# Last image's dynamic filters: one branch of five added up by VectorE in PSUM, its taps spread among the others

## The chip, the cores and the metric

The kernel runs on one core of a Trainium2 chip. The time is that of one execution on the device, in microseconds (us). PE is TensorE (PEld its weight loads), DVE VectorE, ACT ScalarE, POOL GpSimd. SBUF and PSUM are the two on-chip memories of this kernel; its matmuls write to PSUM. The granted clock is TensorE's clock as a share of full speed, as the profile records it; "half clock" is 0.5.

## The reference, cut to what matters

Four images of 256 x 48 x 48 pass through two layers. Layer 0 is a convolution with attention and is not touched. Layer 1 makes, from a 3x3 convolution, 45 weights per pixel (5 branches of 9, a softmax over each 9), and each branch sums nine shifted copies of its input, called taps, under these weights:

```python
for i, d in enumerate((1, 6, 12, 24, 36)):
    w = jax.nn.softmax(guidance[:, 9 * i:9 * (i + 1)], axis=1)
    outs.append(_dyn_branch(x, w, d))      # sum over 9 taps: shifted x * w[:, k]
cat = jnp.concatenate(outs, axis=1)
y = _conv(cat, W_scale, pad=0)             # 1x1, 6*256 -> 256; then batch norm
```

## The kernel before

An image is worked through in six chunks of 8 rows. Each tap takes three engines. TensorE broadcasts the tap's weights over 128 partitions into a PSUM buffer `wb` (a ring of three). VectorE multiplies it with the shifted input into `prod` (a ring of five). POOL adds `prod` to the branch's sum `cat`. When a branch is done, its **mix**, the part of the 1x1 convolution that reads it, is queued and issued on TensorE some six taps later. (The code is cut: `...` and some arguments, `name=` above all, are left out.)

```python
for n in range(len(DILATIONS)):
    cat = work1.tile([P, NH, CH], F32, tag="cat", bufs=CATS)             # CATS = 4
    for k, oy, ox, y0, y1, x0, x1 in taps_of(c, n):
        pw = ps_w.tile([P, 512], F32, tag="w")                           # bufs=3
        nc.tensor.matmul(pw[:, : nr * WW], pick[:, k : k + 1].to_broadcast([2 * NG, P]),
                         w[:, l0 * WW : l1 * WW], start=True, stop=True)
        if k % 9 == 4:
            nc.vector.tensor_tensor(accv, wb, src, ALU.mult)             # first tap, into cat
        else:
            prod = work1.tile([P, NH, CH], F32, tag="prod", bufs=PRODS)  # PRODS = 5
            nc.vector.tensor_tensor(pv, wb, src, ALU.mult)
            nc.gpsimd.tensor_tensor(dst, dst, pv, ALU.add)
        ...
        pump()            # issues queued TensorE work: mixes, guidance steps, layer 0
    for o in range(NH):   # one queue entry for each output half
        queue.append((tap + PRODS + 1, mix(c, n + 1, o, lambda i, cat=cat: cat[:, i, :])))

def pump():
    while owed > 0:
        if queue and queue[0][0] <= tap:
            owed -= queue.pop(0)[1]()
            continue
        ...               # else a guidance step of the next chunks, else layer 0
```

A mix is four matmuls, which the trace shows as eight records. In the timelines shown here each engine works through its instructions in the order in which the kernel issued them, so one that waits or takes long holds up those behind it (as the mix of 4.54 us below does). Layer 1 of images 0 to 2 runs beside layer 0 of the next image; that of image 3 runs alone at the end of the program.

## Time and profile before

| | before |
|---|---|
| median of 3 runs when the prediction was made | 3422.59 us (3419.55 to 3422.88) |
| span of the profiled run | 3419.3 us |
| last image's loop, first POOL add to last `y` copy | 283.8 us |
| busy in it: POOL, PE, DVE | 258, 230, 177 us |

I measure "the loop" between two marks in the timeline: the start of POOL's first add and the start of ScalarE's copy of the sixth `y`. (The 281 us of the prediction leave out the last mix; its 231 and 179 us of PE and DVE are those of a window a little longer than the loop.) The start of the loop differs by up to 11 us between profiles of unchanged earlier code, so one profile's loop is compared, not its start or end.

The prediction shows that POOL is the busy engine there.

```profile
3212.94 4.54 PE L990 MATMUL py<-cat,wsc 128*128 128x384 f32 x8 [1.95 <-POOL cat L1060]
```
```profile
3212.92 0.76 DVE L1058 TENSOR_TENSOR prod<-wb,pad 128x576 f32<-128x576 f32 x1 [0.81 <-POOL cat L1060]
3217.76 0.76 DVE L1058 TENSOR_TENSOR prod<-wb,pad 128x576 f32<-128x576 f32 x1 [4.08 <-PE wb L1035]
```

TensorE was in a mix of 4.54 us, made no broadcast, and VectorE stood still for 4.08 us. POOL did not notice: its line of fourteen merged adds runs from 3199.75 to 3222.06 us without a break, on the products waiting in its ring.

### The profile page before, as it was taken

To read this page: it belongs to the slowest core of one execution; us is meant where nothing else is said; L and a number is where in the kernel's file an instruction comes from. 1 tells how busy PE (TensorE), PEld (TensorE's weight loads), DVE (VectorE), ACT (ScalarE), POOL (GpSimd) and SP (SyncE) were. 2 spreads that over 40 slices of the span, in tenths; PEclk is the share of its full clock that TensorE was granted. 3 is DMA by queue.
4 is the path that set the end of the run, shared out by engine and by line. 5 is a ranking of instruction groups with operands and counts; after the bars stand their busy time and mean duration, and the time that the engine had idled before them with its cause. 6 is when DMAs were issued, how large, how long until landed. Compare 5 with 4: busy or idle time off the path is not lost. (4 is left out here: it accounts for less than half of the span.)

```text
span 3419.3 us, 45333 instructions
## 1 busy us (share of the span) xinstructions
PE 3158.2 (92%) x17814; PEld 1363.3 (40%) x17814; DVE 2377.3 (70%) x2837; ACT 1471.5 (43%) x1739; POOL 1041.5 (30%) x793
## 2 busy tenths in 40 slices
PE   7999999999989999999998999999998999987873
PEld 4542222445652222345563222245565222233442
DVE  2059899455659898836557899955555999876655
ACT  0067777300118777600024777730011887750002
POOL 0000000068770000037783000007786000007994
PEclk9999999999999999999999999999999999998876
DMA  3110000000002000000003000000000100022004
GB/s 119 29 27 6 6 10 6 15 24 5 10 14 52 6 6 10 11 28 10 5 10 61 6 6 10 6 6 5 5 10 16 23 6 6 10 81 100 10 5 176
DMA packets 70973, 81.52 MB, mean 24 GB/s; under 512 B 51280, under 2 KB 62048, under 8 KB 67680
## 3 DMA queue, kind: packets, MB, share of 16 engines
q1 hardware_dynamic: 69952, 73.15, 7.5%
q0 software_dynamic: 800, 5.41, 0.4%
q8 instruction: 141, 2.31, 0.3%
q14 instruction: 80, 0.66, 0.1%
HBM read 50.23 MB, written 28.31 MB: 23 GB/s over the span
## 5 line engine op out<-in xcount | busy, mean ns | idle before, releaser
L1060 POOL TENSOR_TENSOR cat<-cat,prod 128x768 f32<-128x768 f32 (+7 forms) x768 | 1034.1, 1352 | 2330.1 <-DVE prod L1058 2288.0
L721 ACT ACTIVATE p<-se 128x1024 f32<-128x1024 f32 (+1 forms) x1440 | 1273.6, 937 | 377.2 <-PE se L709 341.0
L754 DVE TENSOR_TENSOR acc<-acc,p 128x1024 f32<-128x1024 f32 (+1 forms) x1200 | 1250.5, 1112 | 42.0 <-ACT p L721 41.1
L709 PE MATMUL se<-q,k 32*128 32x512 f32 (+1 forms) x5760 | 830.5, 602 | 15.8 <-ACT p L721 12.6
L1058 DVE TENSOR_TENSOR prod<-wb,pad 128x768 f32<-128x768 f32 (+7 forms) x768 | 560.5, 750 | 404.4 <-PE wb L1035 369.8
L737 PE MATMUL num<-p,vT 128*32 128x512 f32 (+1 forms) x5760 | 716.6, 568 | 35.4 <-DVE no L757 35.4
L631 PE MATMUL pc<-pad,wc 128*128 128x384 f32 x1728 | 624.1, 494 | 2.3 <-issue 2.3
L1035 PE MATMUL wb<-w,pick 90*128 90x384 f32 (+3 forms) x888 | 478.7, 563 | 58.6 <-DVE prod L1058 52.2
L709 PEld LDWEIGHTS se<-q,k 32*128 32x128 f32 x5760 | 285.1, 184 | 565.2 <-issue 452.7
L631 PEld LDWEIGHTS pc<-pad,wc 128*128 128x128 f32 x1728 | 317.7, 191 | 219.1 <-issue 47.7
L990 PE MATMUL py<-cat,wsc 128*128 128x384 f32 x960 | 365.9, 511 | 16.7 <-POOL cat L1060 16.7
L737 PEld LDWEIGHTS num<-p,vT 128*32 128x32 f32 x5760 | 114.8, 108 | 529.5 <-issue 464.2
L640 ACT ACTIVATE hid<-pc,bn_t_f,bn_s_f 128x384 f32<-128x384 f32 x48 | 32.2, 672 | 614.5 <-PE pc L631 614.5
L1035 PEld LDWEIGHTS wb<-w,pick 90*128 90x128 f32 x888 | 172.3, 197 | 220.2 <-DVE prod L1058 101.6
L990 PEld LDWEIGHTS py<-cat,wsc 128*128 128x128 f32 x960 | 187.2, 200 | 127.4 <-POOL cat L1060 22.9
L875 PE MATMUL pg<-pad,wcat 128*45 128x384 f32 x864 | 173.1, 514 | 2.5 <-DVE pad L585 2.2
L1050 DVE TENSOR_TENSOR cat<-wb,pad 128x768 f32<-128x768 f32 x120 | 114.6, 955 | 86.9 <-PE wb L1035 86.3
L1005 ACT COPY y<-py 128x768 f32<-128x768 f32 x24 | 19.2, 799 | 317.4 <-PE py L990 317.4
L651 PE MATMUL pq<-hid,wqkv 128*128 128x384 f32 x384 | 135.0, 486 | 0.0
L679 DVE TENSOR_REDUCE qm<-q 128x1 f32<-128x2304 f32 x8 | 20.4, 2546 | 156.6 <-ACT q L658 156.5
L812 PE MATMUL pp<-ao,wp 128*128 128x384 f32 x192 | 82.2, 559 | 38.0 <-DVE pad L820 37.1
L754 DVE TENSOR_TENSOR acc<-p,p 128x1024 f32<-128x1024 f32 (+1 forms) x80 | 85.8, 1115 | 32.2 <-ACT p L721 32.2
(115 smaller groups left out, 1085.1 us busy)
## 6 DMA issues: line engine op xcount, KB each, us to landing
pad<-in_x SPq DMA_DIRECT2D x14, 1152.0 KB, 14.7
x_d<-pad SPq DMA_DIRECT2D x48, 192.0 KB, 2.5
y_d<-y SPq DMA_DIRECT2D x24, 384.0 KB, 2.7
xst<-in_x SPq DMA_DIRECT2D x18, 384.0 KB, 3.9
y<-y_d SPq DMA_DIRECT2D x3, 2304.0 KB, 19.6
out<-y SPq DMA_DIRECT2D x6, 1152.0 KB, 12.6
x<-x_d SPq DMA_DIRECT2D x2, 2304.0 KB, 24.2
x_first<-in_x SPq DMA_DIRECT2D x2, 1152.0 KB, 7.3
```

Source lines behind the costliest of these rows:

```text
L631: nc.tensor.matmul(pc[:, :CH], wc[:, i, k, o * P : (o + 1) * P], window(gn, i, c * R, k // 3 - 1, k % 3 - 1), start=(i == 0 and k == 0), s ...
L651: nc.tensor.matmul(pq[:, :CH], wqkv[:, i, s, g * P : (g + 1) * P], hid[:, i, cols], start=(i == 0), stop=(i == NH - 1),)
L709: nc.tensor.matmul(ss[j // 2][:, j % 2, :n], k_[r, g, m * P : (m + 1) * P], q[r, g, q0 : q0 + n], start=True, stop=True,)
L721: nc.scalar.activation(p[:, :, :n], ss[pair][:, :, :n], AF.Exp, scale=QS)
L737: nc.tensor.matmul(st["num"][r, :n], vT[:, m, g * P + j * D : g * P + (j + 1) * D], ps[j // 2][:, j % 2, :n], start=(m == 0), stop=(m == N ...
L754: nc.vector.tensor_tensor(a, other, ps[pair][:, :, :n], ALU.add)
L875: nc.tensor.matmul(pg[64 * s : 64 * s + NG, :CH], wcat[:, i, k, :], window(gn, i, (c + s) * R, k // 3 - 1, k % 3 - 1), start=(i == 0 and k ...
L990: nc.tensor.matmul(py[c][:, o, :CH], wsc[:, n * NH + i, o * P : (o + 1) * P], rhs(i), start=(n == 0 and i == 0), stop=(n == len(DILATIONS) ...
L1035: nc.tensor.matmul(pw[:, : nr * WW], pick[:, k : k + 1].to_broadcast([2 * NG, P]), w[:, l0 * WW : l1 * WW], start=True, stop=True,)
L1050: nc.vector.tensor_tensor(accv, wb, src, ALU.mult)
L1058: nc.vector.tensor_tensor(pv, wb, src, ALU.mult)
L1060: nc.gpsimd.tensor_tensor(dst, dst, pv, ALU.add)
```

## The change

Its intent is to relieve POOL in the last image only. Branch 1 (dilation 6) is summed by VectorE in a PSUM accumulator, which ScalarE copies to `cat` at the end, and its nine taps are spread evenly among those of the other branches, so that the two adders work side by side. The core of the diff:

```diff
+        def spread(taps, own):
+            rest = [(n, i) for n in taps if n not in own for i in range(len(taps[n]))]
+            mine = [(n, i) for n in taps if n in own for i in range(len(taps[n]))]
+            both = [((i + 0.5) / len(t), t[i]) for t in (rest, mine) for i in range(len(t))]
+            return [t for _, t in sorted(both)]
...
-                for n in range(len(DILATIONS)):
...
+                own = {1} if b == B - 1 else set()
+                taps = {n: list(taps_of(c, n)) for n in range(len(DILATIONS))}
+                order = spread(taps, own)
+                for n, at in order:
...
+                        acc = cat
+                        if n in own:
+                            acc = ps_c.tile(
+                                [P, 2, 512], F32, tag="acc", name=f"acc_{b}_{c}", bufs=1
+                            )
...
-                            nc.gpsimd.tensor_tensor(dst, dst, pv, ALU.add)
+                        eng = nc.vector if n in own else nc.gpsimd
+                        eng.tensor_tensor(dst, dst, pv, ALU.add)
...
+                        if n in own:
+                            nc.scalar.copy(cat, acc[:, :, :CH])
```

More of the change, by code (lines that the diff above doesn't have):

```diff
@@ L849, in dynamic_filters @@
         def dynamic_filters(b, ao, chunk, norm, other, pools):
-            ps_w, ps_y, ps_m, work1 = pools
+            ps_c, ps_w, ps_y, ps_m, work1 = pools
             gn = pads[b % 2]
@@ L983, in pump, with mix @@
                     owed -= got
-            def mix(c, n, o, rhs):
+            def mix(c, n, o, rhs, last=False):
                 def go():
@@ L994, in go @@
                             start=(n == 0 and i == 0),
-                            stop=(n == len(DILATIONS) and i == NH - 1),
+                            stop=(last and i == NH - 1),
                         )
-                    if n == len(DILATIONS) and o == NH - 1:
+                    if last and o == NH - 1:
                         done(c)
@@ L1025, in dynamic_filters @@
                 w = ready[c]
-                for n in range(len(DILATIONS)):
-                    cat = work1.tile(
-                        [P, NH, CH], F32, tag="cat", name=f"cat_{b}_{c}_{n}", bufs=CATS
-                    )
-                    accv = cat.rearrange("p h (r w) -> p h r w", w=WW)
-                    for k, oy, ox, y0, y1, x0, x1 in taps_of(c, n):
-                        nr, ncol = y1 - y0, x1 - x0
-                        l0, l1 = y0 - c * R, y1 - c * R
-                        pw = ps_w.tile([P, 512], F32, tag="w", name=f"wb_{b}_{c}_{k}")
-                        nc.tensor.matmul(
-                            pw[:, : nr * WW],
-                            pick[:, k : k + 1].to_broadcast([2 * NG, P]),
-                            w[:, l0 * WW : l1 * WW],
-                            start=True,
-                            stop=True,
-                        )
-                        wb = (
-                            pw[:, : nr * WW]
-                            .rearrange("p (r w) -> p r w", w=WW)[:, :, x0:x1]
-                            .unsqueeze(1)
-                            .to_broadcast([P, NH, nr, ncol])
-                        )
-                        src = gn[:, :, 1 + y0 + oy : 1 + y1 + oy, 1 + x0 + ox : 1 + x1 + ox]
-                        if k % 9 == 4:
-                            nc.vector.tensor_tensor(accv, wb, src, ALU.mult)
-                        else:
-                            prod = work1.tile(
-                                [P, NH, CH], F32, tag="prod", name=f"prod_{b}_{c}_{k}", bufs=PRODS
-                            )
-                            pv = prod[:, :, : nr * ncol].rearrange(
-                                "p h (r w) -> p h r w", w=ncol
-                            )
-                            nc.vector.tensor_tensor(pv, wb, src, ALU.mult)
-                            dst = accv[:, :, l0:l1, x0:x1]
-                            nc.gpsimd.tensor_tensor(dst, dst, pv, ALU.add)
-                        tap += 1
-                        owed += NH * nr * ncol * rate
-                        pace[0] += STEPS * 1.15 * NH * nr * ncol * NCK / 2 / TAP_ELEMENTS
-                        pump()
-                    for o in range(NH):
-                        queue.append(
-                            (tap + PRODS + 1, mix(c, n + 1, o, lambda i, cat=cat: cat[:, i, :]))
-                        )
@@ new lines, in dynamic_filters @@
+                own = {1} if b == B - 1 else set()
+                taps = {n: list(taps_of(c, n)) for n in range(len(DILATIONS))}
+                order = spread(taps, own)
+                accs, mixed = {}, []
+                for n, at in order:
+                    k, oy, ox, y0, y1, x0, x1 = taps[n][at]
+                    if at == 0:
+                        cat = work1.tile(
+                            [P, NH, CH], F32, tag="cat", name=f"cat_{b}_{c}_{n}", bufs=CATS
+                        )
[3 more added lines that the diff above has]
+                                [P, 2, 512], F32, tag="acc", name=f"acc_{b}_{c}", bufs=1
+                            )
+                        accs[n] = acc, cat
+                    acc, cat = accs[n]
+                    accv = acc[:, :, :CH].rearrange("p h (r w) -> p h r w", w=WW)
+                    nr, ncol = y1 - y0, x1 - x0
+                    l0, l1 = y0 - c * R, y1 - c * R
+                    pw = ps_w.tile([P, 512], F32, tag="w", name=f"wb_{b}_{c}_{k}")
+                    nc.tensor.matmul(
+                        pw[:, : nr * WW],
+                        pick[:, k : k + 1].to_broadcast([2 * NG, P]),
+                        w[:, l0 * WW : l1 * WW],
+                        start=True,
+                        stop=True,
+                    )
+                    wb = (
+                        pw[:, : nr * WW]
+                        .rearrange("p (r w) -> p r w", w=WW)[:, :, x0:x1]
+                        .unsqueeze(1)
+                        .to_broadcast([P, NH, nr, ncol])
+                    )
+                    src = gn[:, :, 1 + y0 + oy : 1 + y1 + oy, 1 + x0 + ox : 1 + x1 + ox]
+                    if at == 0:
+                        nc.vector.tensor_tensor(accv, wb, src, ALU.mult)
+                    else:
+                        prod = work1.tile(
+                            [P, NH, CH], F32, tag="prod", name=f"prod_{b}_{c}_{k}", bufs=PRODS
+                        )
+                        pv = prod[:, :, : nr * ncol].rearrange("p h (r w) -> p h r w", w=ncol)
+                        nc.vector.tensor_tensor(pv, wb, src, ALU.mult)
+                        dst = accv[:, :, l0:l1, x0:x1]
+                        eng = nc.vector if n in own else nc.gpsimd
+                        eng.tensor_tensor(dst, dst, pv, ALU.add)
+                    tap += 1
+                    owed += NH * nr * ncol * rate
+                    pace[0] += STEPS * 1.15 * NH * nr * ncol * NCK / 2 / TAP_ELEMENTS
+                    pump()
+                    if at == len(taps[n]) - 1:
+                        if n in own:
+                            nc.scalar.copy(cat, acc[:, :, :CH])
+                        mixed.append(n)
+                        for o in range(NH):
+                            queue.append(
+                                (
+                                    tap + PRODS + 1,
+                                    mix(
+                                        c, n + 1, o, lambda i, cat=cat: cat[:, i, :],
+                                        len(mixed) == len(DILATIONS),
+                                    ),
+                                )
+                            )
@@ L1152, in conv_preact_kernel @@
                         ]
-                    dynamic_filters(b - 1, ao, chunk, norm1, other, (ps_w, ps_y, ps_m, work1))
+                    dynamic_filters(b - 1, ao, chunk, norm1, other, (ps_c, ps_w, ps_y, ps_m, work1))
             if b == B:
```

## The prediction

> **What bounds the kernel now.** First I read the page's slices. Layer 1 of image b runs beside layer 0 of image b+1, except for the last image, which runs alone at the end. The change touches only that tail. It shows where POOL is busy after the last stretch of ACT, in slices 37 to 40 (85 us each):
>
> ```profile
> DVE  2059899455659898836557899955555999876655
> ACT  0067777300118777600024777730011887750002
> POOL 0000000068770000037783000007786000007994
> PEclk9999999999999999999999999999999999998876
> ```
>
> POOL reaches 9 only there, and TensorE's granted clock is lowest there. Next I asked for the busy time of each engine in the whole tail loop (first row) and in its six chunks of 8 image rows (the next six), and the waits inside it. The columns are PE, PEld, DVE, ACT and POOL busy us with instruction counts, then PE clock, DMA share and GB/s.
>
> ```profile
> 3088.00:3373.00 285.00, 230.58 (x666) 119.12 (x666) 178.98 (x250) 9.14 (x16) 257.73 (x192) 0.80 0.05 20
> 3091.80:3137.00 45.20, 42.57 (x154) 18.93 (x153) 29.16 (x42) 1.38 (x3) 42.63 (x33) 0.90 0.10 43
> 3137.00:3184.00 47.00, 33.16 (x86) 19.20 (x84) 30.76 (x44) 1.75 (x3) 41.38 (x33) 0.71 0.02 9
> 3184.00:3233.00 49.00, 43.85 (x157) 19.84 (x156) 30.90 (x42) 2.18 (x4) 44.96 (x32) 0.90 0.02 9
> 3233.00:3283.00 50.00, 38.70 (x97) 21.95 (x95) 34.51 (x46) 1.75 (x3) 45.87 (x32) 0.73 0.02 8
> 3283.00:3332.00 49.00, 36.08 (x91) 20.23 (x89) 28.94 (x42) 0.80 (x1) 44.42 (x35) 0.79 0.02 8
> 3332.00:3373.00 41.00, 32.67 (x80) 18.12 (x81) 22.91 (x35) 0.80 (x1) 38.47 (x31) 0.79 0.03 10
> ```
> ```profile
> POOL cat L1060 <- DVE prod L1058: 463.1, 17, 450.6
> ...
> DVE prod L1058 <- PE wb L1035: 60.0, 49, 4.8
> ...
> PE wb L1035 <- DVE prod L1058: 26.2, 42, 2.3
> DVE cat L1050 <- PE wb L1035: 24.1, 14, 4.7
> ```
>
> POOL does 192 adds in the 281 us from 3092 to 3373. Of its wait for VectorE, 450.6 us is the gap before the loop, so only 12.5 us in 16 waits lies inside. Its saturated 6 us slices hold 5.76 us of work for four adds, a cost of about 0.06 us between adds: 257.7 + 192 x 0.06 + 12.5 = 281.7. POOL therefore sets the loop's pace. VectorE (179 us) waits some 84 us for TensorE there; that is slack today. Note chunks 1 and 3 (first and third row of the six): TensorE is 94% and 89% busy. They also carry the 3x3 guidance convolution for the next two chunks, and TensorE had no wait over 0.4 us from 3092 to 3127.
>
> **What the Trainium skill says.** "SBUF — State Buffer", Who interferes with whom: a VectorE instruction with two SBUF inputs contends with a GpSimd instruction that reads SBUF; one with at most one SBUF input outside the 2-port modes does not. That explains the PSUM accumulator: the new add reads one operand from PSUM. The trace agrees: the softmax's copy of 270 elements out of PSUM takes 430 ns beside POOL, the SBUF-to-SBUF cast and copy of as many take 1397 and 1676 ns, but the product of 768 (one operand in PSUM) keeps 949 ns. "GPSIMD Engine Reference", section 3.1: an fp32 tensor_tensor is about 1.96 times slower on GpSimd at 2048 elements. Here, for 768 elements, 1814 against 949 ns, 1.91 times. "TensorE: Matmul & The Clock Gate", Part 1: the array runs at half clock until it has been busy for about 3.4 us. The trace agrees: in the tail's 6 us slices the clock moves between 0.50 and 1.00, and eight mix records take 4.54 us in one place and 2.74 us in another.
>
> **The change, part by part.**
> Only the last image differs (`own = {1}` there). Branch 1, dilation 6, has 48 adds in six chunks: 32 of 672 elements, 10 of 768, 4 of 168, 2 of 192.
> Off POOL, by its rows in the loop (1498, 1814, 511, 589 ns): 47.9 + 18.1 + 2.0 + 1.2 = 69.3 us, with 48 x 0.06 us between them 72 us. POOL keeps 144 adds and about 198 us.
> Onto VectorE, by the rows of the product of the same shapes, which also mix a PSUM and an SBUF input (853, 949, 330, 352 ns): 27.3 + 9.5 + 1.3 + 0.7 = 38.8 us. Each add needs the product just before it; dependent small VectorE instructions follow each other after some 0.03 us, so about 40 us. That the PSUM output costs no more is my assumption. VectorE gets 179 + 40 = 219 us.
> Added to ScalarE: six copies of the accumulator, priced by the y copy of 768 at 0.80 us, 4.8 us in an engine that is 9 us busy in the loop. Beside other work, unless the next chunk's first dilation-6 tap (four taps later, over 2 us) or the mix meets it.
> Moved: the dilation-6 taps go evenly among the others, one in four, and the branch's mix moves behind branches 0, 2 and 3. The built order still shows each mix six taps after its branch. The matmuls remain the same. The tail end is alike: two mixes are left after the last tap in both.
>
> **The sum by chunk.** VectorE's row plus 5.6 us of adds (outer chunks) or 7.3 us (middle ones): 34.8, 38.0, 38.2, 41.8, 36.2, 28.5. POOL: 31.6 to 33.9 in each. So VectorE binds chunks 2, 4, 5 and 6 of six. For chunks 1 and 3 I estimate TensorE from full-clock stretches: a step of four guidance records takes 0.78 us, 18 steps 14 us; 48 mix records at 0.34 us 16.4 us; 37 tap broadcasts at about 0.3 us 11 us; together about 42 us. These two gain little: 42 against 45 and 49. The floor is 42 + 38 + 42 + 42 + 36 + 29 = 229 us, against 281. It would be reached only if VectorE never waited. But a mix holds TensorE for 2.7 us at full and about 5 us at half clock, and three broadcast buffers cover about 2.5 us of products. In the four VectorE chunks there are some 20 mixes; at 0.5 to 2 us exposed, mean 1.2, that is 24 us. So the loop takes about 253 us and gains 28.
>
> **Rivals.**
> (a) The gain is POOL's whole relief, limited by VectorE alone: loop about 225 us, 3367 us. For it: sums of 219 and 198 us. Against: TensorE is already near full in two chunks, and VectorE waits for it 63 times today.
> (b) TensorE replaces POOL: its order mixes behind branch ends, it goes cold in gaps, and the 231 us at a 0.80 clock don't shrink. Loop about 265 to 272 us, 3407 to 3413 us. For it: the two crowded chunks and 84 us of waiting for broadcasts. Against: much of that waiting is TensorE itself waiting for POOL or for products; a faster loop leaves fewer gaps and a warmer array.
> (c) The interleaving backfires: products of both kinds share a ring of five, so POOL has about four adds of lead instead of five, and a VectorE stalled behind POOL delays its own adds too; or the PSUM add is much dearer than a product. At double its price, 40 us more on VectorE: loop about 285 us, within 2% still.
>
> **Range and chances.** 3422.6 - 28 = 3395 us. Low end: stalls almost vanish, gain 45. High end: rival (b), gain 11. A gain over 2% (68 us) would need a loop of 213 us, below VectorE's own sum, so faster gets almost no chance; slower by 2% needs a 350 us loop.
>
> **What would show it.** In the profile after: POOL has 720 adds in all and 144 adds, about 188 us, in the tail; VectorE about 220 us busy there; a new group of 48 VectorE adds with PSUM input and output at some 853 ns for 672 elements; POOL now waiting for products for some 50 us, no longer 12.5; the first and third chunks at 42 us or more, the others nearer 40; a clock above 0.80. Wrong if the loop is shorter than 235 us (TensorE hid better than I think), if the 672-element PSUM add is over 1000 ns, or if the loop shrinks under 10 us, with VectorE waiting over 60 us for broadcasts as today.

## More of the kernel before

One more view shows how a wait looks that costs nothing. These are three answers of the timeline around 3210 us, POOL's, TensorE's and VectorE's: start, duration, instruction, how many merged, and in brackets the idle time before and who ended it.

```profile
3199.75 22.31 POOL L1060 TENSOR_TENSOR cat<-cat,prod 128x672 f32<-128x672 f32 x14
```

## The result, and the profile after

The changed kernel took 3416.12 us (median of 4 runs, 3413.13 to 3421.93), the kernel before beside it 3422.74 us: 6.6 us less, where 28 were forecast. A ratio here is the mean time of one kernel's fast runs over that of the other's in the same rounds, so not quite the ratio of the medians. It is 0.9985, with a 95% interval of 0.9968 to 1.0002, which includes no gain at all. The time lies above the predicted range.

The slices of the page after, as in the prediction:

```profile
DVE  2058999455669898835557899955555999976775
ACT  0067777300118777600024777730012877750002
POOL 0000000068770000037783000007776000005663
PEclk9999999999999999999999999999999999998876
```

POOL fell from 9 to 5 or 6. The clock row is unchanged. The busy row of the loop after (its length first, then PE, PEld, DVE, ACT, POOL, clock):

```profile
3088.20:3368.00 279.80, 226.79 (x664) 118.52 (x662) 210.48 (x296) 13.96 (x22) 189.27 (x144) 0.81 0.03 12
```

The work moved just as computed: POOL from 257.7 to 189.3 us, VectorE to 210.5 us. But 280 us of loop hold it, and no engine is full. The waits in the loop (waiting engine, what it waited for: us in total, times, longest):

```profile
POOL cat L1080 <- DVE prod L1077: 533.3, 48, 453.4
...
DVE prod L1077 <- PE wb L1056: 44.1, 34, 3.6
...
PE wb L1056 <- DVE prod L1077: 35.1, 56, 2.5
...
DVE yst L1014 <- ACT y L1012: 14.1, 5, 6.9
...
DVE acc L1071 <- PE wb L1056: 6.5, 4, 3.7
...
DVE prod L1077 <- POOL cat L1080: 2.3, 4, 1.4
...
DVE cat L1071 <- PE wb L1056: 1.4, 1, 1.4
```

POOL now waits 533.3 - 453.4 = 79.9 us for products. VectorE, which feeds it, waits 44.1 + 6.5 + 1.4 (for first taps) = 52 us for broadcasts, 14.1 us for the copies of `y` (6.9 of them the last one, after all taps) and 2.3 us for POOL. Together with its 210.5 us of work that is the loop. And TensorE in its turn waits for VectorE to free a `wb` buffer: the two wait for each other by turns. The chain of waits through the stretch shows which of them holds the time (its summary by line, shares of the chain):

```profile
by line: PE py L997 38.9%; DVE prod L1077 14.9%; PE wb L1056 12.8%; issue 8.1%; PE pg L882 7.8%; POOL cat L1080 5.9%; DVE cat L1071 2.4%; DVE acc L1080 1.5%; DVE yst L1014 1.5%; PE pw L936 1.2%; ACT y L1012 1.1%; DVE head L927 1.0%; DVE ymv
```

The mixes (`py`) are 38.9% of a window of 282 us, about 110 us. VectorE's products and adds, which I had taken for the bound of four chunks, are under 20%. One mix in the timeline after, in the fifth chunk, with VectorE's and POOL's lines around it:

```profile
3288.41 0.69 PE L1056 MATMUL wb<-w,pick 90*128 90x384 f32 x1 [0.18 <-DVE prod L1077]
...
3288.90 5.32 PE L997 MATMUL py<-pad,wsc 128*128 128x384 f32 x8
3289.27 0.93 DVE L1077 TENSOR_TENSOR prod<-wb,pad 128x752 f32<-128x752 f32 x1
...
3290.11 0.95 DVE L1071 TENSOR_TENSOR cat<-wb,pad 128x768 f32<-128x768 f32 x1
...
3290.98 0.75 DVE L1077 TENSOR_TENSOR prod<-wb,pad 128x576 f32<-128x576 f32 x1
...
3293.45 1.39 PE L1056 MATMUL wb<-w,pick 90*128 90x384 f32 x3
...
3294.59 1.72 DVE L1077 TENSOR_TENSOR prod<-wb,pad 128x768 f32<-128x768 f32 x2 [2.87 <-PE wb L1056]
...
3295.70 1.82 POOL L1080 TENSOR_TENSOR cat<-cat,prod 128x768 f32<-128x768 f32 x1 [1.44 <-DVE prod L1077]
```

Eight mix records at half clock take 5.32 us. VectorE has the three broadcasts of the ring, 2.5 us of products, then stands for 2.87 us; POOL runs dry too. It is the stall seen before at 3217 us, with one difference: the slack that hid it is gone.

### The profile page after: what moved, and what is told of

It is laid out like the page before. It is cut to its first block, busy times and chain, and to the rows that moved or that the text cites. A ratio compares the mean times of both kernels' runs of the same rounds, so it can differ in the third digit from the quotient of the medians.

```text
span 3411.4 us, 45264 instructions
## 1 busy us (share of the span) xinstructions
PE 3150.3 (92%) x17814; PEld 1359.5 (40%) x17814; DVE 2410.1 (71%) x2885; ACT 1475.1 (43%) x1745; POOL 972.3 (29%) x745
## 4 chain that ended last, share of the span: by engine, by line
PE 71%; issue 13%; DVE 12%; ACT 2%; DMA 1%; POOL 1%; DVEq 0%; ACTq 0%; POOLq 0%
PE pc L631 16%; PE se L709 14%; PE num L737 12%; PE py L997 11%; DVE acc L754 5%; PE pg L882 4%; PE wb L1056 4%; PE pq L651 4%; PE den L761 2%; DVE prod L1077 2%; PE pv L669 2%; PE pp L812 2%; ACT p L721 1%; POOL cat L1080 1%; DVE no L757 1%
## 5 line engine op out<-in xcount | busy, mean ns | idle before, releaser
L1080 POOL TENSOR_TENSOR cat<-cat,prod 128x752 f32<-128x752 f32 (+8 forms) x720 | 965.0, 1346 | 2389.8 <-DVE prod L1077 2352.7
L754 DVE TENSOR_TENSOR acc<-acc,p 128x1024 f32<-128x1024 f32 (+1 forms) x1200 | 1250.2, 1111 | 41.7 <-ACT p L721 40.7
```

The lines of the kernel that those rows point to most:

```text
L754: nc.vector.tensor_tensor(a, other, ps[pair][:, :, :n], ALU.add)
L1080: eng.tensor_tensor(dst, dst, pv, ALU.add)
```

## The experiments

The theory, called T in the expectations: TensorE's mix comes as a block, broadcasts stand behind it in order, and three buffers don't cover it, so VectorE and TensorE work by turns. Its rivals: V, VectorE's own work sets the loop; O, the new tap order, which puts mixes together at the chunk's end, costs what the relief gains. All differences act in the last image only.

| run | edit | median us | ratio to before (95%) | loop us | DVE waits for `wb`, us |
|---|---|---|---|---|---|
| before | | 3422.7 | | 283.8 | 88 |
| after | | 3416.1 | 0.9985 (0.9968 to 1.0002) | 279.0 | 55 |
| e1 | after, half the mix matmuls | 3385.8 | 0.9882 (0.9864 to 0.9901) | 244.9 | 26 |
| e2 | before, half the mix matmuls | 3415.5 | 0.9975 (0.9958 to 0.9992) | 278.2 | 52 |
| e3 | order alone | 3425.5 | 1.0004 (0.9988 to 1.0021) | 286.7 | 74 |
| e4 | VectorE adds alone | 3416.4 | 0.9979 (0.9963 to 0.9996) | 277.5 | 52 |
| e5 | before, 5 `wb` | 3422.4 | 0.9995 (0.9978 to 1.0011) | 281.4 | 69 |
| e6 | after, sum in SBUF | 3429.1 | 1.0004 (0.9981 to 1.0027) | 291.7 | 48 |
| e7 | e6, 5 `wb` | 3407.2 | 0.9955 (0.9938 to 0.9972) | 268.4 | 25 |
| e8 | after, 4 pooled `wb` | 3395.6 | 0.9921 (0.9904 to 0.9937) | 260.1 | 36 |
| e9 | after, half mix a tap | 3400.1 | 0.9931 (0.9913 to 0.9948) | 261.5 | 40 |
| e10 | after, one mix matmul a tap | 3383.7 | 0.9884 (0.9862 to 0.9905) | 248.1 | 25 |
| e11 | e8 and e10 | 3377.7 | 0.9867 (0.9849 to 0.9885) | 242.2 | 20 |
| e12 | e6, TensorE kept busy | 3426.7 | 1.0012 (0.9994 to 1.0030) | 284.9 | 40 |
| e13 | before, 5 `wb`, one mix matmul a tap | 3412.7 | 0.9977 (0.9959 to 0.9994) | 279.1 | 49 |
| e14 | e11 without the spreading | 3410.3 | 0.9964 (0.9942 to 0.9986) | 271.6 | 36 |

The last column adds up the three kinds of VectorE wait for a broadcast in one stretch from 3085 us to the end of the loop; it begins a few us ahead of the loop, hence 55 for the 52 us above. Each run had three rounds. e1 to e4 ran in one call, as did e5 to e8, e9 to e12, and e13 with e14; between calls the ratios are compared.

**e1, e2: half of each mix.** Wrong results: the second contraction half is left out, which halves the mix and nothing else.

```diff
+                    few = 1 if b == B - 1 else NH
-                    for i in range(NH):
+                    for i in range(few):
```

> Wrong result on purpose: in the last image each mix keeps only one of its two contraction halves, so 72 of the 144 mix matmuls (144 of 288 records) go; the sequence is otherwise the changed kernel's. Theory T (TensorE and VectorE take turns: while a mix holds TensorE for 2.6 to 5.1 us no tap broadcast is made, and three broadcast buffers don't cover it): the chain's 109 us of mix in the tail roughly halves, the loop falls from 279 to about 235 to 250 us, and the time to about 3375 to 3390 us; VectorE's waits for broadcasts fall from 52 to under 30 us. Rival V (VectorE's own 210 us of work and its order set the loop): under 8 us gained. Rival O (the new tap order costs it): under 8 us gained as well.

> The same cut in the kernel before, wrong result on purpose. All theories: POOL sets that loop, so the time stays within 8 us of before's 3422 us, POOL busy 258 us of the loop. If it gains over 15 us, TensorE was part of the bound before the change already.

The same cut takes 34 us off the loop after (279.0 to 244.9) and 6 off the loop before. VectorE's work in e1 is still 210.5 us, so rival V falls: with the same work it finishes 34 us earlier. The mixes were hardly on the path before and are on it after.

**e3, e4: each part of the change alone.** In e3 the order is new but all adds are on POOL; in e4 VectorE adds in PSUM but branch follows branch.

```diff
# e3
-                        eng = nc.vector if n in own else nc.gpsimd
+                        eng = nc.gpsimd
# e4
-                order = spread(taps, own)
+                order = spread(taps, set())
```

> The new tap order alone, all adds on POOL in SBUF. Theory T and V: POOL still has 192 adds (258 us) and sets the loop, 281 us plus or minus 6, time 3416 to 3430 us. Rival O (the new order, with mixes bunched at the chunk's end, costs by itself): over 8 us slower than before.

> The adds on VectorE in PSUM alone, branch after branch as before. In branch 1 VectorE then has 9 products and 8 adds, about 15 us a chunk in which POOL has only its backlog of some 5 us; POOL's 33 us a chunk plus about 10 us idle make 43 to 46 us a chunk. Theory T: TensorE's mixes meet no denser stretch than before, loop 270 to 290 us, time 3410 to 3432 us. Rival O expects it to beat the changed kernel by over 8 us, as it lacks the spreading.

The order alone costs nothing that the interval separates from zero, and without it the change is as fast as with it. Rival O falls. What is odd is that the spreading, made to let both adders work side by side, gains nothing; e14 returns to it.

**e5 to e8: the number of broadcast buffers.** Before, PSUM has room for two more `wb` buffers in the last image, as e5 shows by running; after, the accumulator takes that room. e6 frees it by summing in SBUF, e7 uses it for `wb`, and e8 keeps the accumulator and lets the softmax's scratch bank and the broadcasts share four buffers.

```diff
# e5, e7
-    name=f"ps_w_{b}", bufs=3, space=PSUM
+    name=f"ps_w_{b}", bufs=5 if b == B else 3, space=PSUM
# e8: bufs=4, and in misc():
+                if b == B - 1:
+                    return ps_w.tile([P, 512], F32, tag="w", name=name)
```

> The kernel before with five broadcast buffers in the last image in place of three (its two other PSUM banks are unused there). POOL sets that loop and waited only 12.5 us for products, so theory T and V expect at most 8 us: 3414 to 3426 us.

> The changed kernel with branch 1 added up by VectorE in SBUF, straight in cat, three broadcast buffers, no ScalarE copy. If two SBUF inputs make VectorE and POOL take turns, the 672-element add is well over 866 ns (1100 to 1500) and POOL's adds lengthen; VectorE's work grows by 10 to 30 us, and the time is 3420 to 3445 us. If sharing costs nothing, 3412 to 3420 us, like the changed kernel.

> The same with five broadcast buffers in the two banks that the accumulator leaves free. Theory T: two more broadcasts ahead cover some 1.7 us more of each of about 30 mixes, so it beats e6 by 15 to 40 us, and VectorE's waits for broadcasts fall below 30 us. Theory V: under 6 us better than e6.

> The changed kernel with PSUM accumulator, and the softmax's scratch bank pooled with the broadcasts: four buffers for both. In chunks 1 and 3 the guidance sum holds one, in the other chunks broadcasts have nearly four. Theory T: 5 to 20 us better than the changed kernel, 3396 to 3411 us. Theory V: within 5 us of it.

The kernel before gains nothing from five. e7 beats e6 by 22 us. e8 beats the changed kernel by some 20 us, a little more than expected: one more buffer is worth three times the change. e6 also prices the choice of PSUM. VectorE's adds of 672 elements in the loop of the changed kernel, then of e6 (count, busy us, mean ns):

```profile
L1080 DVE TENSOR_TENSOR acc<-acc,prod 128x672 f32<-128x672 f32 x32 | 27.7, 866 | 1.1
```
```profile
L1080 DVE TENSOR_TENSOR cat<-cat,prod 128x672 f32<-128x672 f32 x32 | 41.3, 1290 | 1.1
...
L1080 POOL TENSOR_TENSOR cat<-cat,prod 128x576 f32<-128x576 f32 x28 | 44.8, 1601 | 10.9 <-DVE prod L1077 9.2
```

With two SBUF inputs the add takes 1290 in place of 866 ns, and POOL's add of 576 elements 1601 in place of 1403. The PSUM accumulator was right; its price is the room of two `wb` buffers.

**e9, e10: the size of TensorE's blocks.** The same mixes, three buffers, but after each tap only one half mix (e9), or one matmul (e10).

```diff
+                mixes_now = 0
                 while owed > 0:
-                    if queue and queue[0][0] <= tap:
+                    if queue and queue[0][0] <= tap and not (b == B - 1 and mixes_now):
                         owed -= queue.pop(0)[1]()
+                        mixes_now += 1
# e10 besides: one queue entry for each (o, i), a single matmul
```

> The changed kernel, three buffers, but in the last image at most one half of a mix (4 records, 1.3 us at full clock, 2.6 us at half) after each tap, so a broadcast goes out between the halves. Theory T: three buffered broadcasts (about 2.5 us of VectorE work) cover a half, so VectorE's waits for broadcasts fall from 52 to 25 to 40 us and the time by 8 to 25 us, to 3391 to 3408 us. If it is the amount of TensorE work that counts and not its block size, under 5 us.

> The same with one matmul of a mix (2 records, 0.65 us at full clock, 1.3 us at half) after each tap. Theory T: at least as good as e9, 3385 to 3405 us. If the amount counts and not the block size: within 5 us of the changed kernel.

Not one instruction less, yet 16 and 32 us faster than the changed kernel by the medians. The timeline of e10 around a mix, at the start of its fifth chunk:

```profile
3281.56 0.63 PE L1059 MATMUL wb<-w,pick 90*128 90x384 f32 x1
...
3282.03 0.81 PE L999 MATMUL py<-cat,wsc 128*128 128x384 f32 x2
3282.12 2.07 DVE L1080 TENSOR_TENSOR prod<-wb,pad 128x576 f32<-128x576 f32 x3
...
3282.92 0.44 PE L1059 MATMUL wb<-w,pick 90*128 90x384 f32 x1
...
3283.20 0.81 PE L999 MATMUL py<-cat,wsc 128*128 128x384 f32 x2
```

A broadcast, one mix matmul (two records, 0.81 us), a broadcast, one mix matmul: VectorE runs three products in a row meanwhile, with no bracket, so no wait. The block, not the number of TensorE's instructions, was the cost. The same work also runs faster: TensorE is busy 209.3 us in e10's loop against 226.8 for the same matmuls, at a granted clock of 0.87 in place of 0.81. So e10 changed two things at once, the length of the blocks and the clock at which they run; e12 below tries to part them.

**e11: both remedies.** The edits of e8 and e10 together.

> Four pooled buffers (e8) and single mix matmuls (e10) together, the candidate for the best. Theory T: both cover the same stall, so the gains add only in part: 3380 to 3395 us, VectorE waiting under 25 us for broadcasts and then bound by its own 211 us plus the crowded chunks 1 and 3.

It is the best version and beats both kernels: 44 us less than the kernel before. The busy row of its loop, columns as above:

```profile
3089.00:3332.00 243.00, 202.84 (x666) 105.78 (x662) 211.65 (x297) 13.41 (x22) 189.22 (x144) 0.89 0.05 20
```

VectorE and POOL do the same 211 and 189 us of work as in the changed kernel, in 243 us in place of 280. VectorE is now busy 87% of the time. The chain's summary for this stretch no longer has one owner:

```profile
by line: PE py L1001 20.0%; POOL cat L1085 19.4%; DVE prod L1082 18.7%; issue 10.8%; PE wb L1061 10.6%; PE pg L884 8.9%; DVE cat L1076 2.8%; PE pw L938 1.2%; DVE yst L1018 1.2%; DVE acc L1085 1.2%; DVE acc L1076 1.1%; DVE e L920 0.9%; DVE h
```

Where in the loop the gain sits can be read from the spacing of the six `y` copies (the first counted from POOL's first add), in us:

| chunk | 1 | 2 | 3 | 4 | 5 | 6 |
|---|---|---|---|---|---|---|
| before | 46.6 | 52.9 | 46.8 | 48.3 | 48.6 | 40.7 |
| after | 47.3 | 53.6 | 46.9 | 45.4 | 48.0 | 37.9 |
| e11 | 46.6 | 48.8 | 46.4 | 35.0 | 34.4 | 31.1 |
| after, by VectorE's products | 43.6 | 51.0 | 45.3 | 47.7 | 49.7 | 38.9 |
| e11, by VectorE's products | 40.1 | 43.5 | 42.6 | 43.8 | 37.0 | 32.4 |

By the copies the remedies take most from chunks 4 to 6, and chunks 1 and 3, with the guidance convolution, stay as long as they were. But the copies are late marks, because each waits for the chunk's last mix, which e11 issues over more taps. The last two rows count instead from VectorE's first product of a chunk to that of the next (the chunks have 36, 39, 36, 36, 39 and 36 products). By these the remedies take 12.7 us off chunk 5, 7.5 off chunk 2, 6.5 off chunk 6, and also 3.5 and 2.7 off chunks 1 and 3.

**e12: is it the half clock?** A mix at half clock lasts twice as long (5.32 against 2.74 us in the changed kernel), so a colder TensorE could be the real culprit. In e12, on the base of e6, after three taps without other work on TensorE, two unused broadcasts are issued into a free bank (`quiet[0]` counts the taps since the last other work).

```diff
+                    if b == B - 1 and quiet[0] > 2:
...
+                        for _ in range(2):
+                            nc.tensor.matmul(
+                                scratch[0][:, :CH],
+                                pick[:, k : k + 1].to_broadcast([2 * NG, P]),
...
```

> e6 (sum in SBUF, three buffers) with 2 unused broadcast matmuls after each of 66 taps that have had no mix or guidance step for three taps, into a free PSUM bank: to keep TensorE's clock up where it waits for VectorE anyway. The result stays right. If the half clock is a part of the stall (about eleven mixes of 4.2 to 5.1 us in place of 2.6 us in the changed kernel's chain), the granted clock of the tail goes from 0.79 to above 0.85 and the time falls 8 to 25 us below e6's 3429 us. If not, within 5 us of e6 or slower.

Inconclusive. The profile counts 132 more matmul records in the loop, but the clock of the loop only went from 0.80 to 0.84, short of what was expected, and the unused matmuls are themselves 4.1% of the chain, some 12 us. The profiled loop is 7 us shorter than e6's; the timed ratios (1.0012 and 1.0004) show no gain. How much of the stall is the half clock, and how much the length of the block, stays open.

The trace of the changed kernel does show where the stall sits. Thirty of its mixes run in one piece of eight records: nineteen took 2.7 to 2.9 us, eleven 4.2 to 5.3 us. VectorE waits 50.6 us for broadcasts after POOL's first add. If each wait is counted to the TensorE block that it overlaps most, 9.2 us belong to the nineteen, 0.5 us each, and 30.1 us to the eleven, 2.7 us each. So most of the stall lies beside the mixes that ran at or near half clock. That is where it lies, not what a full clock would save: no run changed the clock alone.

**e13, e14: the remedies without the change, and without its order.** e13 is the kernel before with five buffers (e5) and single mix matmuls (e10). e14 is e11 with branch after branch in place of the spread order.

> The kernel before, all adds on POOL, with five broadcast buffers and single mix matmuls in the last image. If POOL alone set the loop before: 3412 to 3424 us, at most 10 us of gain (it waited 12.5 us in all). If the mix blocks were part of the bound before too: 3400 us or less.

> e11 without the spreading: branch 1 in its old place, added up by VectorE in PSUM. In branch 1 VectorE has some 15 us a chunk alone and POOL at most a ring of products, about 5 us, so POOL idles some 10 us in each of six chunks: POOL's 198 us and 60 us make 258 us of loop against e11's 242, so about 3390 to 3400 us. If the spreading is worth nothing: within 5 us of e11's 3378 us.

e13 gains 8.7 us: POOL is still in the way. The change alone gains 6.6, the remedies alone 8.7, both together 44. They stand behind one another: either bound hides the other's relief. e14 answers the oddity of e4. With the blocks in place the spreading was worth nothing (e4 against after); with the blocks split, e11 is 1% of the whole time faster than e14 by the ratios to the kernel before, some 33 us. The expectation missed it: e14's loop is 271.6 us where I had estimated 258. POOL, with 189 us of work, is idle for 82 us of it, not for the 60 that I had priced.

## Why the prediction was wrong, by its own steps

**Right.** The bound before was POOL: relieving TensorE or its buffers (e2, e5, e13) moved the time by under 9 us. POOL's work fell to 189.3 us (188 said). The adds cost VectorE 39.5 us (27.7 + 9.7 + 1.4 + 0.7 by their rows; about 40 said), at 866 ns for the 672-element add (853 said), so the assumption about the PSUM output held. The six copies by ScalarE took 0.80 us each and were in nobody's way. POOL's waits grew, to 79.9 us where some 50 were said. VectorE's 210.5 us are 8 below the 219 said. By the durations of its instructions only 2.5 us of that is other work that got shorter; 1.8 us lies in the window of the 179 us, which is longer than the loop, and most of the rest in neighbouring records that overlap more.

**Wrong.** The failed step is the sum's "In the four VectorE chunks there are some 20 mixes; at 0.5 to 2 us exposed, mean 1.2, that is 24 us", with the 42 us for each crowded chunk before it. The mechanism was the right one, a mix holding TensorE longer than three buffers cover; its size was not. Both factors of the 24 us were too small. The kernel issues six mixes a chunk, so 24 in these four, two of them after the last tap, where the sum counts some 20, and the 33 us measured there are 1.4 us for each. The exposed time has no common mean, either: in the changed kernel's loop it was 0.5 us for a mix of 2.7 to 2.9 us, but 2.7 us for each of the eleven at or near half clock (see e12). With the `y` copies as chunk borders, the busy rows and waits of the changed kernel give this bill in us:

| term | predicted | measured |
|---|---|---|
| VectorE's work in chunks 2, 4, 5, 6 | 145 | 137 |
| its waits for broadcasts there | 24 | 33 |
| its waits for `y` copies there | none | 12 |
| its waits for POOL, rest | none | 3 |
| chunks 1 and 3 | 84 | 94 |
| loop | 253 | 280 |

(Rounded; the unrounded measured terms add up to 280.1.) So the stalls were over a third larger, the wait for `y`, which I take to be the same queueing of mixes seen from the other side (no run tests it), was left out (6.9 us of it at the very end, where the two marks for the loop's end account for about 3), and the crowded chunks took 47 us each. TensorE is busy 43.6 and 42.5 us in those two, as I had estimated, but I gave them no idle time at all. Whether the blocks cost these 10 us too depends on where the chunk's border is drawn: by the `y` copies e11 does not shorten the two, by VectorE's products it takes 6 us off them. That split stays open.

e1, e8 and e10 show that the blocks, with the clock at which they run, are the cause of the excess: with the same VectorE work, each takes 19 to 34 us off the loop. e10's 31 us is more than the whole excess over the prediction's 253, so the stall also lengthened what the bill counts under other terms. Of the prediction's own signs of being wrong, one half came true: the loop shrank by 4.8 us, under 10, but with 52 us of waits for broadcasts and not over 60.

**The rival that came nearest** was (b), at 3407 to 3413 us, still too low. What I held against it, that much of the waiting was TensorE itself waiting for POOL, was half right. The mix's wait for POOL's sums inside the loop did nearly vanish (12.7 us before, 1.0 after). But VectorE's waits for broadcasts only fell from 88 to 55 us, because they come from the blocks, and the array did not get warmer (0.80 before, 0.81 after). Rival (a) fell for the reason given; of (c), the PSUM add was not dear, and VectorE waited only 2.3 us for POOL.

## What to carry to other kernels

A wait that costs nothing today is the next bound once the busy engine is relieved: take its longest single wait from the timeline and ask whether the ring of buffers behind it covers that, not just its sum. Where short producer instructions share an in-order queue with long blocks, split the blocks or add a buffer together with the change; here neither the change (6.6 us) nor the remedies (8.7 us) paid alone, and both gave 44 us. Spreading the work between the two adders paid here only once the engine that feeds both delivered evenly (e4 and e14).

## What the Trainium skill lacked or had wrong

- No page names the stall behind a block on an in-order engine. "Perfetto Trace Analysis", Optimization Strategy, says that a repeating gap can mean too few buffers; that fits e8 (one more buffer, 279.0 to 260.1 us of loop). That the same gap shrinks with three buffers too when four matmuls are issued one at a time between the short ones (e10, 248.1 us, no instruction less) is not there.
- "VectorE: DVE Perf Modes", The TRN2 errata, gives costs from SBUF to SBUF and from PSUM to SBUF, none from PSUM to PSUM. Here an in-place PSUM add of 672 elements with one SBUF input took 866 ns, the 768-element one 966 ns.
- "TensorE: Matmul & The Clock Gate", Part 1, ties full clock to about 3.4 us of sustained work and half clock to an idle window of that length, and does not say how dense the work has to be. In the loop of the changed kernel the clock fell to half 13 times; before eight of them TensorE had no idle gap over 1.2 us in the last 3.4 us and was busy for 40 to 73% of it. And 132 more matmul records raised the mean granted clock of a loop only from 0.80 to 0.84 (e12 against e6), while a finer interleaving of the same matmuls raised it from 0.81 to 0.87 (e10) and 0.89 (e11).
